# Layer 0: the q projection of the next image moved ahead of the mixing in the steps behind an image's last scores

## The chip, the cores and the metric

The kernel runs on one core of one Trainium2 chip. The metric is the device time of one execution in microseconds (us). The median of three runs is compared.

## The reference

The network has four layers, all of the form x = x + layer(group_norm(x)), on an image tensor of 4 images, 512 channels and 32x32 positions (1024 tokens), all in f32. Layer 0, in which the change lies, is an attention whose heads are mixed before the softmax:

```python
q, k, v = w_q @ xf, w_k @ xf, w_v @ xf              # 8 heads of 64 channels, 1024 tokens
attn = einsum('bhdq,bhdT->bhqT', q, k) * scale
attn = einsum('gh,bhqT->bgqT', w_head, attn)        # every head becomes a sum over all 8
attn = softmax(attn, axis=-1)
attn = (attn - mean) / sqrt(var + EPS) * in_gamma + in_beta   # one mean and var per image and head
out = einsum('bhqT,bhdT->bhqd', attn, v).reshape(b, t, c) @ w_proj.T + b_proj
```

Layer 1 is a small gate per channel, layer 2 a plain attention, and layer 3 a read of a memory of 2048 rows by the eight best matches. They are not touched.

## The kernel before

Layer 0 handles one image after the other (`for b in range(B)`). An image is cut into 32 steps of 32 queries each (`STEPS` = 32). A block of 32 queries goes through these stages, spread over several steps of the loop:

- `scores(b, s, n)` multiplies q and k for two halves of the keys (L467). ScalarE copies the result out of PSUM into the tile `ss` (L473). After the second half, eight DMAs (four issued by SyncE, four by GpSimd, L482) carry `ss` into `s2` with the heads brought next to each other on the partitions.
- Two steps later (`MIX` = 2), `mix(b, s - 2)` multiplies `s2` with the head weights (L493), `exps` takes the exponentials on ScalarE (L500), `turn_keys` transposes 32x32 blocks on VectorE (L506), and `reduce` takes sums and squares there (L521).
- Seven steps later (`LAG` = 7), `apply(b, s - 7)` multiplies a quarter of the keys of a group of four blocks with v and adds them up in the one PSUM bank `pv_bank` (L532). After the fourth quarter `take_out` copies the bank out on ScalarE (L592), and the next group may start in it. `scale` on GpSimd (L605) and a store follow.

Because of these lags seven steps, 32 to 38, have no scores any more: they only mix (steps 32 and 33, for the blocks 30 and 31) and apply. In the first four of them, 32 to 35, the kernel also makes the q projection of the next image, one of four blocks of 128 channels in each step. The function passed in as `piece` does this: `take_q(b + 1, m, s + 1)` runs 8 matmuls of 128x512 (shown as 16 records, L192, through `project`), and `put_q` copies the result with ScalarE (L292). Behind the last image the projection is that of layer 2, `take_q2`, and its result is taken by VectorE (L989). The weights come in four blocks of columns (`load_columns`, L261), asked for in steps 30 to 33 on ScalarE's DMA queue. The normalised input of the next image, `xn_all`, gets its last quarter from ScalarE at the end of step 31 (L397).

The big PSUM tiles are three, `pairs[0..2]`, used in turn: the projection of step s writes `pairs[(s + 1) % 3]`, and the mixing of step s writes `pairs[(s + 2) % 3]` and `pairs[s % 3]`.

`mid` stands between the mixing and the `piece` of a step. In the steps 32 to 38 it takes one part of the gate of layer 1 for the image before (`gating`, L145, L155, L886 and so on), so it is empty for the first image.

The order is written by hand: `pin` keeps an instruction in program order on its engine, and nearly all of layer 0 is pinned. So TensorE, ScalarE and VectorE each take the work in the order of the code below.

Of the kernel before, what the change touches and what calls it, by code (L numbers as in the profile page):

```python
# [41 lines left out]
def fast_net(ctx: ExitStack, tc: tile.TileContext, a: dict, out: bass.AP, flag: bass.AP):  # L42
# [181 lines left out]
    STEPS = T // NS  # L224
# [193 lines left out]
    def take_v(b, t):  # L418

        I = img[b]  # L420
        if t == 0:
            I["v"] = big("v", f"v0_{b}").rearrange("p k (i c) -> p (k i) c", c=C)
        ps = small_ps(f"v_{b}_{t}")
        for k in range(KC):
            pin(nc.tensor.matmul(  # L425
                ps, I["xn"][:, k, t * P:(t + 1) * P], I["w_v"][:, k, :],
                start=(k == 0), stop=(k == KC - 1),
            ))
        pin(nc.scalar.copy(I["v"][:, t, :], ps))
# [11 lines left out]
    def sum_v(b):  # L441

        I = img[b]
        vk = I.pop("vk")
        ps = small_ps(f"vt_{b}")
        for g in range(NH):
            for half in range(2):
                pin(nc.tensor.matmul(
                    ps[half * HD:(half + 1) * HD, g:g + 1],
                    vk[:, g * HD:(g + 1) * HD], ones[:, 0:1], start=True, stop=True))  # L450
        vsum = I["vsum"] = small.tile([P, NH], F32, tag="vsum", name=f"vsum{b}")
        pin(nc.vector.tensor_scalar_mul(vsum, ps[:, 0:NH], float(T)))
# [3 lines left out]
    def scores(b, s, n):  # L456


        I = img[b]
        q, k_ = I["q"], I["k"]  # L460
        if n == 0:
            I["ss", s] = eight_k([P, 2, T], f"ss_{b}_{s}", s % 2)
        ss = I["ss", s]
        sc = pairs[(s + n) % 3]
        for m in range(KC):
            for r in range(2):
                pin(nc.tensor.matmul(  # L467
                    sc[m * NS:(m + 1) * NS, r, :],
                    q[r * HD:(r + 1) * HD, m, s * NS:(s + 1) * NS],
                    k_[r * HD:(r + 1) * HD, m, n * NB:(n + 1) * NB],  # L470
                    start=True, stop=True,
                ))
        pin(nc.scalar.copy(ss[:, :, n * NB:(n + 1) * NB], sc))  # L473
        if n == 0:
            return
        s2 = I["s2", s] = apool.tile([P, 2, T], F32, tag="s2", bufs=2, name=f"s2_{b}_{s}")
        del I["ss", s]
        for r in range(2):
            for i in range(2):
                for side in range(2):  # L480
                    m = 2 * side + i
                    pin(relays[side].dma_start(  # L482
                        out=s2[2 * m + r::NH], in_=ss[m * NS:(m + 1) * NS, r, :]))
# [5 lines left out]
    def mix(b, s):  # L489
        s2 = img[b].pop(("s2", s))  # L490
        for t in range(4):
            for r in range(4):
                pin(nc.tensor.matmul(  # L493
                    mixed(s, r // 2)[t * NS:(t + 1) * NS, r % 2, :].rearrange("p (qq k) -> p qq k", qq=2),
                    wmix[r * NS:(r + 1) * NS], s2[r * NS:(r + 1) * NS, :, t * NK:(t + 1) * NK],
                    start=True, stop=True,
                ))

    def exps(s, half):
        pin(nc.scalar.activation(  # L500
            e[:, half].rearrange("p r qq k -> p (r qq k)"), flat2(mixed(s, half)), AF.Exp))

    def turn_keys(s, half):

        j, i = divmod(s, 4)
        pin(nc.vector.transpose(  # L506
            eT[:, j % 2].rearrange("p b (qq i r) x -> p i r qq b x", qq=2, i=4)[
                :, i, 2 * half:2 * half + 2],
            e[:, half].rearrange("p r qq (b x) -> p r qq b x", x=NS),
        ))  # L510

    def reduce(b, s, half):

        I = img[b]
        j, i = divmod(s, 4)
        if i == 0 and half == 0:
            I["st", j] = apool.tile([P, 4, 4, 2, 6], F32, tag="st", bufs=2, name=f"st_{b}_{j}")
        st = I["st", j]
        for r in range(2):
            for qq in range(2):  # L520
                pin(nc.vector.bn_stats(st[:, i, 2 * half + r, qq, :], e[:, half, r, qq, :]))  # L521

    def apply(b, s):

        I = img[b]
        j, part = divmod(s, 4)
        pv = pv_bank.rearrange("p (gp q) -> p gp q", q=P)
        for t in (2 * part, 2 * part + 1):
            for gp in range(KC):
                for r in range(2):  # L530
                    g = 2 * gp + r
                    pin(nc.tensor.matmul(  # L532
                        pv[r * HD:(r + 1) * HD, gp, :],
                        I["v"][:, t, g * HD:(g + 1) * HD],
                        eT[:, j % 2, t, :, 4 * g:4 * g + 4],
                        start=(t == 0 and gp == 0), stop=(t == TC - 1),
                        skip_group_check=True,
                    ))
# [51 lines left out]
    def take_out(b, j):  # L590
        pv = img[b]["pv"] = apool.tile([P, KC, P], F32, tag="o1", name=f"pv_{b}_{j}")
        pin(nc.scalar.copy(pv.rearrange("p gp q -> p (gp q)"), pv_bank))  # L592
# [94 lines left out]
    def piece_out(b, m, n):  # L687
        pin(nc.sync.dma_start(
            out=x1[b][:, m, n * NB:(n + 1) * NB], in_=img[b].pop(("xr", m, n))))
# [18 lines left out]
    def unit(i):  # L708

        return i // 2 % KC, i // (2 * KC)  # L710
# [569 lines left out]
    def step(b, s, mid, piece):  # L1280


        I = img[b]
        old = s - MIX
        mixing = 0 <= old < STEPS
        js, at = divmod(s - SUM, 4)
        if js >= TC:
            js, at = TC - 1, s - SUM - 4 * (TC - 1)
        summing = js >= 0
        j, part = divmod(s - LAG, 4)  # L1290
        tiled = 0 <= j < TC
        putting = b > 0 and OUT <= s < OUT + 16
        if b > 0 and OUT < s <= OUT + 16 and s % 2 == 0:
            piece_out(b - 1, *unit(s - 2 - OUT))
        if s == 0:
            take_v(b, 0)
        if s < STEPS:
            scores(b, s, 0)
            early(b, s)
            scores(b, s, 1)  # L1300
        else:
            early(b, s)
        if summing and at == 2:
            next(I["tail"])
        if putting:
            mid(b, s)
        if s >= MIX and "late" in I:
            turn_keys(I["late"], 1)
            reduce(b, I.pop("late"), 1)
        if summing and at == 0:  # L1310
            I["rest"] = I.pop("tail", None)
            I["tail"] = sums(b, js)
            next(I["tail"])
        if s == LAG:
            sum_v(b)
        if tiled:
            apply(b, s - LAG)
        else:
            piece(b, s)
        if mixing:  # L1320
            mix(b, old)
            exps(old, 0)
            exps(old, 1)
            turn_keys(old, 0)
        if tiled and part == 3:
            take_out(b, j)
        if b > 0 and OUT <= s + 1 < OUT + 16 and s % 2:
            image_piece(b - 1, *unit(s + 1 - OUT))
        if not putting:
            mid(b, s)  # L1330
        if s < STEPS:
            feed(b, s)
        if tiled:
            piece(b, s)
        if mixing:
            reduce(b, old, 0)
            I["late"] = old
        if summing and at >= 2:
            next(I["tail"])
        if summing and at == 0 and js > 0:  # L1340
            next(I["rest"])
        if tiled and part < 3 and j > 0:
            next(I["scale"])
        if tiled and part == 3:
            I["scale"] = scale(b, j)
# [5 lines left out]
    def early(b, s):  # L1351

        for load in state["plan"].get(s, ()):
            load()

    def mid(b, s):
        before = b - 1
        if b > 0:
            if s == 3:
                state["norm"] = instance_norm(before)  # L1360
            if 3 <= s < 7:
                next(state["norm"])
            if s in (OUT - 2, OUT - 1, OUT + 6, OUT + 7):
                norm_quarter(before, s % 2 + 2 * (s > OUT))
        if TC < s <= TC + 4 or s in (NEXT - 4, NEXT, NEXT + 2, NEXT + 3):
            next(state["ahead"])
        next(state["behind"], None)

    def piece(b, s):
        if s < TC - 1:  # L1370
            take_v(b, s + 1)
        elif b > 0 and OUT <= s < OUT + 16:
            put_quarter(b - 1, s - OUT)
# [10 lines left out]
    for b in range(B):  # L1384
# [8 lines left out]
        for s in range(STEPS):  # L1393
            step(b, s, mid, piece)
# [854 lines left out]
```

## Time and profile before

| | |
|---|---|
| median of 3 runs | 2590.84 us (2585.73 to 2593.91) |
| the profiled execution | 2590.89 us, its span 2589.2 us |
| TensorE busy | 2534.9 us, 98% of the span |
| VectorE, GpSimd, ScalarE busy | 1549.0, 1204.8, 988.4 us |
| share of TensorE in the chain that ended last | 74% |
| mixing on TensorE (L493) | 160.6 us busy, 9.3 us idle before it |

The span is the time from the first to the last instruction of the profiled execution; its own device time is 1.7 us longer. The idle time before a group is what its engine stood still just before the instructions of that group. Records of matmuls overlap, since TensorE is pipelined, so the distance from one group's start to the next group's start is a better measure of what a group costs than its length.

The steps 32 to 38 lie, on TensorE, at about 268 to 315 us for the first image, 557 to 603 us for the second, 847 to 894 us for the third and 1138 to 1185 us for the fourth.

### The profile page before, as it was taken

How to read it: one execution, taken by the hardware profiler on the slowest of the kernel's cores; microseconds unless marked ns; L12 is line 12 of the kernel's file. 1: busy time of each engine (PE TensorE's matmuls, PEld its weight loads, DVE VectorE, ACT ScalarE, POOL GpSimd, SP SyncE). 2: the span in 40 equal slices, each digit the busy share in tenths (PEclk: the TensorE clock that was granted, in tenths of full speed). 3: DMA queues.
4: the chain of work that ended last, by engine and by line, in shares of the span. 5: the costliest groups of instructions: out<-in, count | busy, mean ns of one | idle time of the engine just before them, and what ended most of it. 6: DMA issues, size and time to landing. Idle time of an engine off the chain costs nothing.

```text
span 2589.2 us, 47488 instructions
## 1 busy us (share of the span) xinstructions
PE 2534.9 (98%) x18438; PEld 1164.4 (45%) x18438; DVE 1549.0 (60%) x2668; ACT 988.4 (38%) x1165; POOL 1204.8 (47%) x1700
## 2 busy tenths in 40 slices
PE   8999999999999999999999999999999999999998
PEld 3344534544355534545533433443343344444445
DVE  4599348871788338880366147226514647787885
ACT  1467336651666236651152145025314622121211
POOL 3266315552456425543284047017404617656665
PEclk9999999999999999999999999999999999999999
DMA  2578448872698439883300120030012036767665
GB/s 82 144 208 233 119 120 233 234 205 81 179 242 235 111 95 224 234 253 122 130 17 24 68 91 21 29 134 25 13 57 82 22 113 183 224 181 222 183 189 169
DMA packets 186969, 358.22 MB, mean 138 GB/s; under 512 B 32873, under 2 KB 96361, under 8 KB 183026
## 3 DMA queue, kind: packets, MB, share of 16 engines
q1 hardware_dynamic: 105504, 175.57, 21.9%
q0 software_dynamic: 49152, 142.79, 20.3%
q10 hardware_dynamic: 32082, 36.76, 5.0%
q8 instruction: 148, 2.42, 0.4%
q14 instruction: 83, 0.68, 0.1%
HBM read 186.96 MB, written 33.82 MB: 85 GB/s over the span
## 4 chain that ended last, share of the span: by engine, by line
PE 74%; issue 10%; POOL 8%; DMA 3%; ACT 2%; DVE 2%; SPq 0%; POOLq 0%; ACTq 0%; DVEq 0%
PE pair L192 10%; PE sc_c L1027 9%; PE pv_c L1064 8%; PE pv L532 8%; POOL got L1204 7%; PE pair L467 6%; PE pair L493 5%; PE pt L425 4%; PE p L192 4%; PE pt L721 4%; PE k L192 3%; PE q L192 3%; PE v L204 3%; DMA s<-ss 2%; ACT e L500 2%
## 5 line engine op out<-in xcount | busy, mean ns | idle before, releaser
L482 POOL DMA_DIRECT2D s<-ss x512 | 259.2, 513 | 396.2 <-PE pair L493 106.4
L506 DVE STREAM_TRANSPOSE eT<-e 128x1024 f32<-128x1024 f32 x256 | 316.4, 1236 | 176.9 <-ACT e L500 176.4
L1204 POOL DMA_INDIRECT got<-in_mem,ix x256 | 279.7, 1093 | 213.3 <-DVE tmx L1210 144.3
L1021 ACT ACTIVATE eT<-sc_c 128x1024 f32<-128x1024 f32 x256 | 247.8, 1022 | 289.9 <-PE sc_c L1027 213.6
L521 DVE BATCH_NORM_STATS2 st<-e 128x6 f32<-128x256 f32 x1024 | 350.7, 404 | 0.0
L500 ACT ACTIVATE e<-pair 128x1024 f32<-128x1024 f32 x256 | 251.1, 1022 | 181.7 <-PE pair L493 145.8
L1045 POOL TENSOR_TENSOR e<-eT 128x1024 f32<-128x1024 f32 x96 | 236.2, 2464 | 158.2 <-ACT eT L1021 123.6
L467 PE MATMUL pair<-k,q 64*32 64x512 f32 x4096 | 267.4, 598 | 12.8 <-ACT e L500 12.8
L473 ACT COPY ss<-pair 128x1024 f32<-128x1024 f32 x256 | 247.2, 1019 | 74.2 <-PE pair L467 36.6
L532 PEld LDWEIGHTS pv<-eT,v 128*64 128x64 f32 x4096 | 221.1, 137 | 76.0 <-issue 59.4
L532 PE MATMUL pv<-eT,v 128*64 128x128 f32 x4096 | 250.7, 276 | 4.3 <-ACT pv L592 4.3
L1046 DVE TENSOR_TENSOR eT<-eT,e 128x1024 f32<-128x1024 f32 x96 | 138.7, 1445 | 179.8 <-POOL e L1045 179.7
L1027 PE MATMUL sc_c<-q,k 64*128 64x512 f32 x1024 | 238.7, 606 | 2.3 <-DVE xr L684 2.3
L1041 POOL TENSOR_TENSOR eT<-eT 128x1024 f32<-128x1024 f32 x32 | 80.3, 2509 | 334.8 <-ACT eT L1021 330.9
L1064 PE MATMUL pv_c<-eT,v 128*64 128x512 f32 x1024 | 233.1, 597 | 1.5 <-DVE eT L1121 1.5
L493 PE MATMUL pair<-s,wmix 32*32 32x512 f32 x4096 | 160.6, 599 | 9.3 <-DMA s<-ss 8.3
L1251 DVE SCALAR_TENSOR_TENSOR acc<-got,et,acc 128x512 f32<-128x512 f32 x210 | 157.9, 752 | 7.5
L1027 PEld LDWEIGHTS sc_c<-q,k 64*128 64x128 f32 x1024 | 94.3, 187 | 132.2 <-issue 73.3
L1184 ACT COPY att<-at 128x1024 f32<-128x1024 f32 (+1 forms) x65 | 64.9, 999 | 217.7 <-PE at L1179 216.7
L467 PEld LDWEIGHTS pair<-k,q 64*32 64x32 f32 x4096 | 57.0, 105 | 179.9 <-ACT e L500 86.6
L1064 PEld LDWEIGHTS pv_c<-eT,v 128*64 128x64 f32 x1024 | 68.0, 137 | 138.4 <-issue 136.8
L1179 PE MATMUL at<-memT,xn_d 128*128 128x512 f32 x256 | 120.7, 594 | 0.0
(295 smaller groups left out, 3306.1 us busy)
## 6 DMA issues: line engine op xcount, KB each, us to landing
s<-ss SPq DMA_DIRECT2D x512, 128.0 KB
s<-ss POOLq DMA_DIRECT2D x512, 128.0 KB
rb<-r POOLq DMA_DIRECT2D x64, 128.0 KB
o<-o SPq DMA_DIRECT2D x32, 256.0 KB
xr<-in_x ACTq DMA_DIRECT2D x32, 256.0 KB
x<-xr SPq DMA_DIRECT2D x32, 256.0 KB
xr_c<-x SPq DMA_DIRECT2D x32, 256.0 KB
rb_c<-r SPq DMA_DIRECT2D x64, 128.0 KB
```

Source lines behind the costliest of these rows:

```text
L192: pin(nc.tensor.matmul(ps[:, n, :], w[:, k, m * P:(m + 1) * P], rhs(k, n), start=(k == 0), stop=(k == KC - 1),))
L467: pin(nc.tensor.matmul(sc[m * NS:(m + 1) * NS, r, :], q[r * HD:(r + 1) * HD, m, s * NS:(s + 1) * NS], k_[r * HD:(r + 1) * HD, m, n * NB:(n ...
L482: pin(relays[side].dma_start(out=s2[2 * m + r::NH], in_=ss[m * NS:(m + 1) * NS, r, :]))
L493: pin(nc.tensor.matmul(mixed(s, r // 2)[t * NS:(t + 1) * NS, r % 2, :].rearrange("p (qq k) -> p qq k", qq=2), wmix[r * NS:(r + 1) * NS], s ...
L500: pin(nc.scalar.activation(e[:, half].rearrange("p r qq k -> p (r qq k)"), flat2(mixed(s, half)), AF.Exp))
L506: pin(nc.vector.transpose(eT[:, j % 2].rearrange("p b (qq i r) x -> p i r qq b x", qq=2, i=4)[:, i, 2 * half:2 * half + 2], e[:, half].rea ...
L521: pin(nc.vector.bn_stats(st[:, i, 2 * half + r, qq, :], e[:, half, r, qq, :]))
L532: pin(nc.tensor.matmul(pv[r * HD:(r + 1) * HD, gp, :], I["v"][:, t, g * HD:(g + 1) * HD], eT[:, j % 2, t, :, 4 * g:4 * g + 4], start=(t == ...
L1021: pin(nc.scalar.activation(e, scs[len(es)], AF.Exp))
L1027: pin(nc.tensor.matmul(sc[:, r, :], I["k"][r * HD:(r + 1) * HD, m, t * P:(t + 1) * P], I["q"][r * HD:(r + 1) * HD, m, n * NB:(n + 1) * NB] ...
L1064: pin(nc.tensor.matmul(pv[r * HD:(r + 1) * HD, :], I["v"][:, t, h * HD:(h + 1) * HD], e[:, r, :], start=(t == 0), stop=(t == TC - 1),))
L1204: pin(nc.gpsimd.indirect_dma_start(out=got[:, i, :], out_offset=None, in_=a["mem"], in_offset=bass.IndirectOffsetOnAxis(ap=ix[:, i:i + 1], ...
```

## The change

In the steps from `STEPS` on, `piece` is called right behind `apply`, ahead of `mix`, `exps`, `turn_keys`, `take_out` and `mid`. In all other steps the order stays as it is. In the steps 36 to 38 the `piece` is empty, so the steps 32 to 35 alone change.

```diff
         if tiled:
             apply(b, s - LAG)
-        else:
+        if not tiled or s >= STEPS:
             piece(b, s)
         if mixing:
             mix(b, old)
@@ -1330,7 +1330,7 @@
             mid(b, s)
         if s < STEPS:
             feed(b, s)
-        if tiled:
+        if tiled and s < STEPS:
             piece(b, s)
         if mixing:
             reduce(b, old, 0)
```

## The prediction

> **What bounds the kernel now.** I read the page first: busy times, then the chain.
>
> ```profile
> PE 2534.9 (98%) x18438; PEld 1164.4 (45%) x18438; DVE 1549.0 (60%) x2668; ACT 988.4 (38%) x1165; POOL 1204.8 (47%) x1700
> PE 74%; issue 10%; POOL 8%; DMA 3%; ACT 2%; DVE 2%; SPq 0%; POOLq 0%; ACTq 0%; DVEq 0%
> ```
>
> TensorE is busy almost throughout and holds most of the chain. A reordering can then only win where TensorE stands still, and costs wherever it makes TensorE stand still anew. So I went to the timeline of TensorE over the steps 32 to 35 of the first image. Columns: start, length, line, shapes, records, in brackets the idle time ahead and what ended it.
>
> ```profile
> 267.85 1.97 PE L532 MATMUL pv<-eT,v 128*64 128x128 f32 x32
> 271.99 1.15 PE L493 MATMUL pair<-s,wmix 32*32 32x512 f32 x32 [2.17 <-DMA s<-ss]
> 273.07 8.83 PE L192 MATMUL pair<-xn_all,w_q 128*128 128x512 f32 x16
> 281.83 1.97 PE L532 MATMUL pv<-eT,v 128*64 128x128 f32 x32
> 283.73 1.14 PE L493 MATMUL pair<-s,wmix 32*32 32x512 f32 x32
> 284.80 7.13 PE L192 MATMUL pair<-xn_all,w_q 128*128 128x512 f32 x16
> 291.86 1.97 PE L532 MATMUL pv<-eT,v 128*64 128x128 f32 x32
> 293.76 7.13 PE L192 MATMUL pair<-xn_all,w_q 128*128 128x512 f32 x16
> 300.82 1.97 PE L532 MATMUL pv<-eT,v 128*64 128x128 f32 x32
> 302.72 7.13 PE L192 MATMUL pair<-xn_all,w_q 128*128 128x512 f32 x16
> ```
>
> Apply, mixing, projection is the order of steps 32 and 33; steps 34 and 35 have apply and projection. The mixing of step 32 waits for the relayed scores of block 30; that of step 33 waits for nothing. The same place in the other three images:
>
> ```profile
> 557.35 1.97 PE L532 MATMUL pv<-eT,v 128*64 128x128 f32 x32
> 559.79 1.15 PE L493 MATMUL pair<-s,wmix 32*32 32x512 f32 x32 [0.48 <-DMA s<-ss]
> ...
> 847.41 1.97 PE L532 MATMUL pv<-eT,v 128*64 128x128 f32 x32
> 851.09 1.15 PE L493 MATMUL pair<-s,wmix 32*32 32x512 f32 x32 [1.71 <-DMA s<-ss]
> ...
> 1137.68 1.97 PE L532 MATMUL pv<-eT,v 128*64 128x128 f32 x32
> 1141.56 1.15 PE L493 MATMUL pair<-s,wmix 32*32 32x512 f32 x32 [1.91 <-DMA s<-ss]
> ```
>
> The first projection of image 0 also took 8.83 us where the others took 7.13. The table of stretches says why (its columns: stretch, length, busy time of PE, PEld, DVE, ACT, POOL, then granted clock, DMA share, GB/s):
>
> ```profile
> 269.60:273.00 3.40, 1.23 (x36) 0.27 (x32) 3.33 (x9) 1.22 (x2) 3.27 (x6) 1.00 1.05 239
> 273.00:276.40 3.40, 3.40 (x20) 1.35 (x6) 3.40 (x8) 2.05 (x2) 1.38 (x2) 0.56 1.04 295
> ```
>
> The clock fell to about half right behind the wait. The DMA share of 1.05 says why the scores are late: the DMA engines are full here. Last, ScalarE from step 33's q copy on:
>
> ```profile
> 291.97 1.01 ACT L292 COPY q<-pair 128x1024 f32<-128x1024 f32 x1 [4.96 <-PE pair L192]
> 293.93 0.59 ACT L592 COPY pv<-pv 128x512 f32<-128x512 f32 x1 [0.95 <-PE pv L532]
> 300.93 1.01 ACT L292 COPY q<-pair 128x1024 f32<-128x1024 f32 x1 [6.41 <-PE pair L192]
> ```
>
> The copy of the pv bank in step 34 (293.93) now runs under the projection of that step (293.76 to 300.82). It is off TensorE's path only because it stands ahead of the q copy.
>
> **What the Trainium skill says.** "TensorE: Matmul & The Clock Gate", Part 1: an idle window of about 3.4 us halves the clock, and windows run freely. The trace agrees in kind: 0.56 over 3.40 us. But the gap was 2.17 us, less than a full window, and gaps of 1.71 and 1.91 us in images 2 and 3 left their projections at 7.11. The same page, "Step-by-step: what each phase is for", says that TensorE can pull weight loads ahead but keeps matmuls in program order, and that it alone of the engines reorders. The timelines of TensorE and ScalarE agree: both follow the code. So a wait stops all matmuls behind it, and a ScalarE copy behind another waits for it.
>
> **What goes away (step 32).** From apply's start to the mixing's start is 1.90 us undisturbed (281.83 to 283.73). In step 32 it is 4.14, 2.44, 3.68 and 3.88 us in the four images: 2.24 + 0.54 + 1.78 + 1.98 = 6.54 us too long. With the projection ahead, the mixing starts 7.06 us after apply's end (length of a projection from start to start, 284.80 to 291.86), which covers all four. In image 1, L145 waits a further 0.2 us for VectorE; that goes too, as L145 then also comes 7 us later. The slow clock cost (281.83 - 273.07) - 7.06 = 1.70 us. Together **8.45 us**. Otherwise the same three groups run in another order, for which I take no cost; a different handover between shapes could be 0.1 us for each of 8 steps, either way.
>
> **Does the projection wait instead?** It needs three things. Weights: by the DMA semaphores' updates in the trace, the first block of columns (L261, issued at 259.58) had landed at 264.62; in the other images at 552.81, 843.96 and 1133.92; the projection would start at about 269.8, 559.3, 849.3 and 1139.6. Input: the last quarter of xn ends on ScalarE at 270.82 (L397, 269.58 plus 1.24), about 1.05 us after apply, but only the fourth of the eight matmuls (two records each, so 7.06 / 8 = 0.88 us) reads it, 2.65 us in. The margin is 1.6 us; waiting for the whole tile at the first matmul would cost 1.05 us each, 4.2 us in all. PSUM: the projection's pair was freed by exponentials of the step before. For step 33: the mixing of step 32 starts at Q, the end of the projection; the exponential starts 1.33 us later (273.32 against 271.99) and ends at Q + 2.35. TensorE is there at Q + 1.07 + 1.90 = Q + 2.97. Margin 0.6 us; I cost it at nothing. The q copy stands ahead of that exponential on ScalarE, from Q + 0.11 to Q + 1.12, and is done before the exponential may start. The mixing of block 31 needs that step's second exponential, over 6 us earlier.
>
> **What is moved past what.** A projection is 16 records of TensorE with their weight loads and one copy; it issues no DMA. On ScalarE's queue the load of the last weight block (281.94) comes forward or stays, and is needed only at 302. SyncE and GpSimd are not passed, but wait: GpSimd's L605 needs the pv copy, 8 us later in step 34, and its next work behind that starts at 310.69, so that is covered. On VectorE the transposes of block 31 ended at 289.82 (the last one starts at 288.58 and takes 1.23), 6.1 us after their mixing's start (283.73). That mixing now starts at 269.75 + 7.06 + 1.07 + 1.90 + 7.06 = 286.84, so they end near 292.9; the apply that reads all of them starts at 296.9 at the earliest: margin 4 us. In the last image VectorE takes q (1.28 us) ahead of transposes whose exponentials come later still: nothing.
>
> **What is added (step 34).** Now `take_out` stands behind the q copy on ScalarE. The next apply (step 35) is the first of a new group and needs the bank. With TensorE's next start at 300.82: q copy at 300.93, second copy 0.92 us behind it (two ScalarE instructions of 1.02 take 1.94 together), 0.59 long, TensorE 0.05 later: 302.49. So **1.67 us** of new idle time in image 0. In images 1 and 2 the small L155 (0.25 us) falls into it: 1.42 each. In the last image q is copied by VectorE (L989), ScalarE is free, and the cost is 0. Sum: 1.67 + 2 x 1.42 = **4.5 us**. Bounds: 0 if the copy goes ahead after all, 4.5 + 3 x 1.70 = 9.6 if the clock falls behind each.
>
> **Sum.** -8.45 + 4.5 = -3.95 us. Against the profiled 2590.89 this is 2586.9; the median, 2590.84, stands at the same place.
>
> **Rivals.**
> *Only the gain:* the pv copy does not bind, 2590.84 - 8.45 = 2582.4. For it: TensorE waited for L592 only 4.3 us in all. Against it: the order of the code.
> *Slower, by the clock:* in step 34 each of three new gaps lets the clock fall for one window at 1.70 us. -8.45 + 4.5 + 5.1 = +1.1, so 2592.0; if it lasts two windows each, 2597. It decides between a gap that did no harm (1.91) and one that did (2.17), and on how it lies in the window; 1.67 speaks against it.
> *The wait changes its name:* the projection waits for all of xn, +4.2: 2591.1. Against it: the input is written and read by quarters.
> *It does nothing measurable,* because the relays' lateness reappears at a later mixing. Against it: the relays of block 31 had landed at 276.53, and its mixing would come at 287: it stays at 2586.9 then.
>
> **Numbers.** The forecast gets 0.62, only the gain 0.14, the clock 0.13, the renamed wait 0.11. 0.3% (7.8 us) is about what a measurement of this kernel can tell from no change. Most of "only the gain" and the low edge of the forecast lie below 2583.1: 0.20. Above 2598.6 lie the worst of the clock case and what I don't see, unpinned work of later layers among it: 0.09. The rest, 0.71, is within. Range 2581.5 to 2594.0: from a little below the full gain to the clock case with the spread of the runs.
>
> **What would show it.** Right: no `DMA s<-ss` wait at the mixing of steps 32, projections at 7.1, and `ACT pv L592` ahead of step 35's apply at 1.4 to 1.7 us in three images, none in the fourth. Wrong: a wait at L192 for `ACT xn_all L397` or a DMA, a granted clock of 0.5 behind step 34, or no wait at L532.

## The result, and the profile after

| | before | after |
|---|---|---|
| median of 11 runs | 2590.49 us | 2585.75 us |
| ratio to before, 95% interval | | 0.9976 (0.9966 to 0.9987) |
| the profiled execution, and its span | 2590.89, 2589.2 us | 2587.30, 2585.5 us |
| mean granted TensorE clock of the profiled execution | 0.998 | 0.999 |

The ratio of 0.9976 is 6.2 us of 2590 (3.4 to 8.8 us); the medians lie 4.7 us apart, the means 4.3 us and the two profiled executions 3.6 us. The forecast was 2586.9 us, 3.95 us under the kernel before, which lies within that interval. A second set of 9 runs, made beside the first experiments, gave 0.9968 (0.9955 to 0.9982), 8.3 us (4.7 to 11.7 us), which is more than the forecast.

The page of the kernel after, busy times and chain by engine:

```profile
PE 2533.4 (98%) x18438; PEld 1162.9 (45%) x18438; DVE 1548.0 (60%) x2668; ACT 986.9 (38%) x1165; POOL 1199.9 (46%) x1700
PE 74%; issue 8%; POOL 7%; DMA 7%; ACT 2%; DVE 1%; SPq 0%; POOLq 0%; ACTq 0%; DVEq 0%
```

TensorE still does the same 18438 matmul records in nearly the same busy time (2533.4 against 2534.9 us), and still carries the chain. Totals can't show a change of this size; the stage does. The timeline of TensorE over steps 32 to 35 of the first image, kernel after:

```profile
268.30 1.97 PE L532 MATMUL pv<-eT,v 128*64 128x128 f32 x32
270.20 7.13 PE L192 MATMUL pair<-xn_all,w_q 128*128 128x512 f32 x16
277.26 1.14 PE L493 MATMUL pair<-s,wmix 32*32 32x512 f32 x32
278.34 1.97 PE L532 MATMUL pv<-eT,v 128*64 128x128 f32 x32
280.23 7.13 PE L192 MATMUL pair<-xn_all,w_q 128*128 128x512 f32 x16
287.30 1.14 PE L493 MATMUL pair<-s,wmix 32*32 32x512 f32 x32
288.37 1.97 PE L532 MATMUL pv<-eT,v 128*64 128x128 f32 x32
290.27 7.13 PE L192 MATMUL pair<-xn_all,w_q 128*128 128x512 f32 x16
298.99 1.97 PE L532 MATMUL pv<-eT,v 128*64 128x128 f32 x32 [1.59 <-ACT pv L592]
300.89 7.13 PE L192 MATMUL pair<-xn_all,w_q 128*128 128x512 f32 x16
```

Three things are to be seen. First, the mixing of step 32 (277.26) has no wait ahead of it, and neither has the projection (270.20). Second, all four projections take 7.13 us: none runs at the slow clock. Third, the apply of step 35 (298.99) has a wait that was not there. ScalarE shows why, in the same kernel:

```profile
297.44 1.01 ACT L292 COPY q<-pair 128x1024 f32<-128x1024 f32 x1 [6.86 <-PE pair L192]
298.35 0.59 ACT L592 COPY pv<-pv 128x512 f32<-128x512 f32 x1
```

The pv copy waits its turn behind the q copy, and the apply follows it by 0.05 us (298.35 + 0.59 = 298.94). The apply of step 35 in images 1 and 2, and in the last image, from the timelines of TensorE after:

```profile
586.61 1.97 PE L532 MATMUL pv<-eT,v 128*64 128x128 f32 x32 [1.47 <-ACT pv L592]
...
877.53 1.97 PE L532 MATMUL pv<-eT,v 128*64 128x128 f32 x32 [1.47 <-ACT pv L592]
...
1166.54 1.97 PE L532 MATMUL pv<-eT,v 128*64 128x128 f32 x32
```

Two more waits, and none in the last image, where VectorE takes q.

The stage can be summed from start to start, from the apply of step 32 to the first k projection behind step 38 (times in us):

| image | before | after | difference | the prediction's terms |
|---|---|---|---|---|
| 0 | 267.85 to 315.32 | 268.30 to 313.48 | -2.29 | -2.24 - 1.70 + 1.67 = -2.27 |
| 1 | 557.35 to 603.09 | 555.61 to 602.04 | +0.69 | -0.54 - 0.2 + 1.42 = +0.68 |
| 2 | 847.41 to 894.11 | 846.53 to 892.96 | -0.27 | -1.78 + 1.42 = -0.36 |
| 3 | 1137.68 to 1185.29 | 1137.08 to 1182.63 | -2.06 | -1.98 |

The four sum to -3.93 us, against -3.95 in the prediction. For these stages of these two executions the account closes. That the whole spans differ by nearly the same amount (3.7 us) is in part luck: by the starts and ends in the table, the time outside the stages grew by 1.27 us up to the end of the last stage and shrank by 1.04 us behind it. In that last part, which the change does not touch, the two executions differ in the clock. The first matmuls of layer 2's attention wait 2.3 us in both:

```profile
1273.44 8.83 PE L1027 MATMUL sc_c<-q,k 64*128 64x512 f32 x32 [2.32 <-DVE xr L684]
...
1270.78 7.14 PE L1027 MATMUL sc_c<-q,k 64*128 64x512 f32 x32 [2.31 <-DVE xr L684]
```

The first line is of the kernel before, the second of the kernel after. In the 3.40 us from these starts the granted clock was 0.51 before and 1.00 after. So one pair of executions can't settle the size of the change, and the question stays why the second set shows more than the forecast.

### The profile page after: what moved, and what is told of

Same layout as the page of the kernel before. It is cut to its first block, busy times and chain, and to the rows that moved or that the text cites. A ratio compares the mean times of both kernels' runs of the same rounds, so it can differ in the third digit from the quotient of the medians.

```text
span 2585.5 us, 47491 instructions
## 1 busy us (share of the span) xinstructions
PE 2533.4 (98%) x18438; PEld 1162.9 (45%) x18438; DVE 1548.0 (60%) x2668; ACT 986.9 (38%) x1165; POOL 1199.9 (46%) x1700
## 4 chain that ended last, share of the span: by engine, by line
PE 74%; issue 8%; POOL 7%; DMA 7%; ACT 2%; DVE 1%; SPq 0%; POOLq 0%; ACTq 0%; DVEq 0%
PE pair L192 10%; PE sc_c L1027 9%; PE pv_c L1064 9%; PE pv L532 8%; POOL got L1204 7%; PE pair L467 6%; PE pair L493 5%; PE pt L425 4%; PE pt L721 4%; PE p L192 3%; PE k L192 3%; PE q L192 3%; PE v L204 3%; DMA got<-in_mem,ix 3%; DMA s<-ss 3%
## 5 line engine op out<-in xcount | busy, mean ns | idle before, releaser
L473 ACT COPY ss<-pair 128x1024 f32<-128x1024 f32 x256 | 247.2, 1020 | 78.6 <-PE pair L467 37.5
L1027 PE MATMUL sc_c<-q,k 64*128 64x512 f32 x1024 | 237.2, 602 | 2.4 <-DVE xr L684 2.3
L1027 PEld LDWEIGHTS sc_c<-q,k 64*128 64x128 f32 x1024 | 93.5, 186 | 131.7 <-issue 72.0
```

The costliest lines, as they stand in the source:

```text
L1027: pin(nc.tensor.matmul(sc[:, r, :], I["k"][r * HD:(r + 1) * HD, m, t * P:(t + 1) * P], I["q"][r * HD:(r + 1) * HD, m, n * NB:(n + 1) * NB] ...
```

## The experiments

Each is compared with the kernel before on the same chip. Where means are given, they are means over all its runs, and "clock" is the mean granted TensorE clock of these runs. By my estimate from these figures, a clock of 0.999 over 2590 us stands for 2.6 us lost by a TensorE that is always busy.

**The changed kernel again, and its parts.** The yardstick of the first group:

> The changed kernel once more, as the yardstick of this group. My account (a saving of 8.45 us at the mixing of step 32, a cost of 4.5 us at the apply behind step 34): 3.9 us under the kernel before. If the change gains elsewhere too, as the 4.7 us between the medians and the ratio of 0.9976 leave open: 6 us or more under it.

Measured: 0.9968 (0.9955 to 0.9982), median 2583.35 us, 8.3 us: more than my account gives. Where the rest comes from is taken up below, with step 32 alone.

The projection ahead only where there is a mixing (this edit and those below are against the kernel before unless said otherwise; `...` stands for lines left out):

```diff
-        else:
+        if not tiled or STEPS <= s < STEPS + MIX:
             piece(b, s)
...
-        if tiled:
+        if tiled and not (STEPS <= s < STEPS + MIX):
             piece(b, s)
```

> The projection stands ahead only in steps 32 and 33, where there is a mixing; steps 34 and 35 keep the old order. My account: the whole saving and none of the cost, 8.45 us under the kernel before and 4.5 us under the changed one; no wait of the apply for ACT pv L592 over 1 us. Rival (the pv copy's place costs nothing in the end, since the saved time is waited for later): the same as the changed kernel.

Measured: 0.9959 (0.9944 to 0.9974), median 2578.57 us, 4.8 us under the changed kernel's median. The waits of TensorE for the pv copy are 4.3 us in 12 places with a longest of 1.0, as in the kernel before; in the kernel after they are 8.9 us in 15 places. So the cost is close to the forecast 4.5 us, and the saving, 12.4 us by the means, is more than forecast.

The complement, with the condition `s >= STEPS + MIX` in both places:

> The projection stands ahead only in steps 34 and 35; steps 32 and 33 keep the old order. My account: only the cost, 4.5 us over the kernel before, in three waits of 1.4 to 1.7 us for ACT pv L592, none behind the last image; the mixing of step 32 waits as before. Rival: no difference from the kernel before.

Measured: 1.0021 (1.0010 to 1.0032), mean 2596.97 against 2591.76 us: 5.2 us slower (2.6 to 8.3 by the interval). The rival, no difference, falls. Its timeline of TensorE in the first image has both waits at once:

```profile
267.01 1.97 PE L532 MATMUL pv<-eT,v 128*64 128x128 f32 x32
272.06 2.02 PE L493 MATMUL pair<-s,wmix 32*32 32x512 f32 x32 [3.08 <-DMA s<-ss]
274.01 7.71 PE L192 MATMUL pair<-xn_all,w_q 128*128 128x512 f32 x16
...
302.31 1.97 PE L532 MATMUL pv<-eT,v 128*64 128x128 f32 x32 [1.59 <-ACT pv L592]
```

The apply's wait is the same 1.59 us as in the kernel after. The mixing's wait, in the old order of step 32, is 3.08 us here and was 2.17 in the profile before.

**Whose place costs.** The changed order in all four steps, with the q copy of step 34 (`m == 2`) on another engine; this edit is against the changed kernel:

```diff
-    def put_q(q, m):
+    def put_q(q, m, ahead=False):
+        if ahead:
+            return lambda ps: pin(nc.vector.tensor_copy(q[:, m, :], ps))
         return lambda ps: pin(nc.scalar.copy(q[:, m, :], ps))
...
-        project(I["w_q"], tokens(I["xn"]), m, at, put_q(I["q"], m))
+        project(I["w_q"], tokens(I["xn"]), m, at, put_q(I["q"], m, m == 2))
```

> The changed order in all four steps, but the q copy of step 34 is made by VectorE and not by ScalarE. My account (the cost is the pv copy queued behind the q copy on ScalarE): the cost is gone, 8.45 us under the kernel before, and the pv copy follows the apply of step 34 within 1 us. Rival (the cost comes from the projection's place on TensorE, whichever engine copies): as the changed kernel, 3.9 us under.

Measured: 0.9958 (0.9945 to 0.9971), median 2578.93 us, the same as without the move in step 34. ScalarE of this kernel (its lines are two further down in the file, so L594 is the pv copy):

```profile
286.30 1.94 ACT L502 ACTIVATE e<-pair 128x1024 f32<-128x1024 f32 x2 [0.23 <-PE pair L495]
288.12 0.59 ACT L594 COPY pv<-pv 128x512 f32<-128x512 f32 x1
304.06 1.01 ACT L294 COPY q<-pair 128x1024 f32<-128x1024 f32 x1 [15.34 <-PE pair L192]
```

The pv copy now comes right behind the apply of step 34 (286.03 on TensorE), under the projection, and the apply of step 35 has no wait:

```profile
294.99 1.97 PE L534 MATMUL pv<-eT,v 128*64 128x128 f32 x32
```

So the cost is not the projection's place on TensorE but the q copy's place on ScalarE: shown.

**Which step saves.** The condition `s == STEPS`, and in another kernel `s == STEPS + 1`:

> Only in step 32 does the projection stand ahead of the mixing. My account: the whole saving comes from this step, since only its mixing waits for the relayed scores: 8.45 us under the kernel before. Rival (both steps with a mixing take part): half of that or less.

Measured: 0.9953 (0.9940 to 0.9966), median 2578.84 us, mean 2578.54 against 2590.66: 12.1 us under the kernel before.

> Only in step 33 does the projection stand ahead of the mixing. My account: nothing, within 1 us of the kernel before, and the mixing of step 32 waits as before. Rival (the order in step 33 saves or costs by itself, by the handover between shapes or by exponentials that come later): 2 us or more either way.

Measured: 0.9999 (0.9987 to 1.0010). So step 32 makes the whole saving, and step 33 nothing that can be told (3 us either way). Its size is 12 us (8.8 to 15.5) and not 8.45. Two things can make up the difference.

First, the wait varies from execution to execution. Three profiled kernels have the old order in step 32. What lies between the starts of apply and mixing beyond the undisturbed 1.90 us, summed over the four images: 6.54 us before, 7.42 in the kernel that moves step 33 only (2.29, 1.80, 2.24, 1.09), 11.80 in the one that moves steps 34 and 35 only (3.15, 4.14, 1.81, 2.70). The mean is 8.6. It may be high, since the last two executions took 4.3 and 7.3 us more than the means of their kernels. The profile names other releasers than the relays for three of these twelve waits (`ACT xn_all L397`, or "issue"); by the semaphores' updates in the traces the last relay had landed 0.4 to 0.7 us before the mixing there too, as it had where the relays are named.

Second, the clock. In these three profiles it falls in or behind one, two and three of the four waits. Averaged over runs, the granted clock is 0.9977 in the kernel before (40 runs) and 0.9992 with step 32 moved (5 runs): 0.0015 of 2590 us, 3.9 us. Together 8.6 + 3.9 = 12.5 us, against 12.1 measured. The same sum for the change as it was made: 8.6 less the 4.5 of step 34 is 4.1; its clock is 0.9986 in the first set of runs and 0.9989 in the second, so 2.4 to 3.1 us; 6.5 to 7.2 us, between the two measured figures of 6.2 and 8.3. The sums agree better than a mean of three profiles and the clock of five runs can promise. That all of the 3.9 us lies at step 32 is not shown: these three profiles hold two or three slow stretches elsewhere in the kernel too (in the kernel before at about 1273 and 2577 us), and the profile with step 32 moved holds none but at its very end.

**Why the relays are late.** The kernel before, with less in the DMA engines ahead of them:

```diff
-        plan |= {NEXT + 2 + m: [load_columns(b, key, a[key], m)] for m in range(KC)}
+        plan |= {NEXT + 3 + m: [load_columns(b, key, a[key], m)] for m in range(KC)}
```

> The kernel before, with the four weight columns of the next projection asked for one step later each (steps 31 to 34). My account of why the relayed scores of block 30 are late (the DMA engines are full, share 1.05): 256 KB less stand ahead of them, about 1 us at the 239 GB/s of that stretch, so the waits at the mixing of step 32 fall by about 1 us each where they were 1.7 to 2.2, and the kernel is 2 to 4 us faster. Rival (a fixed latency of the relays from the last scores on): the waits stay as they are.

Measured: 0.9976 (0.9968 to 0.9984), 6.2 us, more than the 2 to 4 expected and as much as the change itself. Step 32 loses 1.37, 2.10, 0.86 and 1.33 us in its profile, 5.66 in all, 2.9 under the mean of the three above; the clock of its runs is 0.9987, 2.5 us better than before. A latency that is fixed from the last scores on would not shorten when a load of weights is put off. From the end of the copy of block 30's last scores (L473) to its mixing it was 10.50, 11.33, 11.18 and 11.26 us in the four images of the profile before, and is 9.64, 11.49, 10.26 and 10.73 us here. It is not fixed, and three of the four are shorter, so that rival falls; the forecast fall of about 1 us for each wait is not seen in every image. How much of the wait is the bytes ahead in the engines and how much the rate they share is not told apart.

Both remedies at once:

> The projection ahead of the mixing in step 32 only, and the weight columns asked for one step later each: both remedies for the late relays at once. My account: they cure the same wait, so the second adds nothing, 12 us under the kernel before as with the first alone; and the projection, which now starts at about 268 us in the first image, comes close to the landing of its first weights (268.7 for a load asked for in step 31 in the profile before), so a wait of up to 1 us at L192 in each image can appear, for a result up to 4 us worse than the first alone. Rival (the two gains add up): 18 us under the kernel before.

Measured: 0.9966 (0.9957 to 0.9975), 8.8 us under the kernel before: the gains do not add up to the 18 us of the rival, and the result is no better than with step 32 alone. TensorE at the projection of step 32, first and last image:

```profile
268.31 7.10 PE L192 MATMUL pair<-xn_all,w_q 128*128 128x512 f32 x16 [0.91 <-DMA w_q<-in_w_q]
...
1132.77 7.10 PE L192 MATMUL pair<-xn_all,Wq 128*128 128x512 f32 x16 [1.26 <-DMA Wq<-in_Wq]
```

With its weights a step later the projection itself has to wait. This is the wait that the prediction ruled out by the landing times; it comes when the weights are asked for one step later.

**How long a gap lowers the clock.** The changed kernel, with the q copy of step 34 made twice by ScalarE, the second time over the first:

> The changed kernel, with the q copy of step 34 made twice in a row by ScalarE behind the first three images. My account: the wait for the pv copy grows by 0.92 us in each of three images, to about 2.6, 2.4 and 2.4 us; 2.8 us over the changed kernel by the waits alone. If gaps of 2 us and more bring the clock down as in the profile before: up to 1.7 us more for each that lies in one window of the clock, and the granted clock shows 0.5 behind it. Rival (such gaps never lower the clock, the slow stretch before had another cause): 2.8 us and no more.

Measured: 0.9995 (0.9985 to 1.0006), mean 2589.95 us. The two sets of the changed kernel have a mean of 2584.74, so the doubling costs about 5.2 us; these sets stood in other groups of runs, where the kernel before had means of 2590.1 and 2591.8 against 2590.7 here. From start to start the gaps grow by 1.05 us each (the start of the projection to the start of the next apply is 9.77 us, against 8.72 after), 3.15 in all; the clock is 0.9977 against 0.9988, a further 2.7 us. The table of stretches around the gap of image 2 (columns as in the prediction):

```profile
870.60:874.00 3.40, 3.40 (x9) 1.49 (x9) 1.13 (x4) 0.00 (x0) 1.01 (x4) 1.00 0.00 0
874.00:877.40 3.40, 0.88 (x10) 0.56 (x10) 0.16 (x1) 2.51 (x3) 1.52 (x3) 1.00 0.00 0
877.40:880.80 3.40, 3.40 (x33) 3.07 (x29) 0.00 (x0) 0.00 (x0) 1.44 (x2) 0.52 0.00 0
```

A stretch with TensorE busy for 0.88 of 3.40 us is followed by one at 0.52, in which the apply took 3.33 us where it takes 1.97. The DMA share is 0.00 here, so full DMA engines are not needed for a slow clock. In this profile only one of the three gaps (2.63, 2.52 and 2.52 us) lowered the clock. So the rival, that such gaps never do it, falls; and the price is a chance for each gap, not a fixed sum.

## Why the prediction was right, and where it was short

- **The bound.** TensorE carried the time, and only its gaps moved. Held.
- **What goes away in step 32.** The mechanism held in each of the four images to 0.1 us between the two profiled executions, and step 32 alone makes the saving. But the term was mis-sized: 6.54 us came from one execution, where three profiles give 6.5 to 11.8 us.
- **The slow clock, 1.70 us.** This was the step that failed in size. I counted the one slow stretch that the profile before happened to hold in these stages. Over the runs the clock of the kernel before stands for 2590 x 0.0023 = 6.0 us lost in the whole kernel, and with step 32 moved 3.9 of them are won back, in the stages or elsewhere. The page's row of granted clock, in tenths, shows none of this.
- **Does the projection wait instead?** It did not, by any of the three needs. The weights' lead was needed: with the weights a step later a wait of 0.9 to 1.3 us appeared in two images of that profile.
- **What is added in step 34.** 1.67 and twice 1.42 us forecast; from start to start it is 8.72 - 7.06 = 1.66 us in image 0, and 1.42 in images 1 and 2 with L155's 0.24 taken off; none in the last. Its cause was shown twice, by leaving the step alone and by copying q on VectorE.
- **Rivals.** "Only the gain" was wrong for this change: the new waits are there. The clock case did not come about (no slow stretch behind step 34 in either of its two profiles), though with the doubled copy one of three gaps brought it. The argument against it, that 1.67 us is shorter than a gap that did no harm (1.91), does not hold as a rule, since a wait of 1.53 us brought a slow stretch in another profile (shown in the last section). That none came in six gaps may be luck in part. The renamed wait and "nothing measurable" are excluded by the timeline after.
- **The range.** Both medians of the changed kernel lie within 2581.5 to 2594.0, below its middle, which fits the terms that were sized too small. That the first lies only 1.2 us from the forecast 2586.9 is partly luck: by the means against the kernel before of the same set, the change won 4.3 us in the first set and 8.4 us in the second.

The versions that leave step 34 in the old order, or copy its q on VectorE, beat both kernels, with medians of 2578.6 to 2578.9 us.

## What to carry to other kernels

A block of independent work put in front of a matmul that waits for a transfer hides the wait; but the block's copy out of PSUM goes into a queue too, and what stands behind it there (here a copy that frees a bank) is the price. Look up the queue of every engine that the moved block uses, not only the one where the wait was. And size a wait that ends with a DMA from several executions: the same four waits gave 6.5 us in one profile and 11.8 in another, with a slow clock behind one of them and behind three.

## What the runs showed of the hardware that was not expected

- A gap on TensorE that is well under 3.4 us was enough for a stretch of about 3.4 us at half clock, if not each time, and the length of the gap alone does not decide. Such stretches stand behind waits of 2.17 us (kernel before) and 2.52 us (doubled copy), while waits of 1.71 and 1.91 us left the next projection at 7.11 us, and waits of 2.52 and 2.63 us in the profile with the doubled copy did no harm either. In the kernel that moves step 33 only, a wait of 1.53 us ahead of an earlier mixing was followed by one:

```profile
1010.21 3.04 PE L493 MATMUL pair<-s,wmix 32*32 32x512 f32 x32 [1.53 <-DMA s<-ss]
...
1007.80:1011.20 3.40, 1.87 (x22) 0.81 (x16) 2.99 (x8) 1.02 (x2) 3.07 (x7) 1.00 0.96 189
1011.20:1014.60 3.40, 3.40 (x33) 1.45 (x32) 0.14 (x1) 2.10 (x3) 1.72 (x4) 0.51 0.81 192
```

- One and the same gap is hit or missed. The 2.3 us wait ahead of layer 2's attention (L1027, lower in the versions with added lines), which no version touches, stands in all eleven profiles. Behind it the granted clock was 0.50 to 0.54 in four of them, and the matmuls took 8.69 to 8.83 us; it was 1.00 in seven, and they took 7.14 us.
- The granted clock of the kernel before differs between executions, from 0.995 to 0.999 over 40 runs, with a mean of 0.9977. Over these runs a clock lower by 0.001 goes with about 2.7 us more (correlation -0.78), so a good part of the scatter between runs goes with the clock. That gaps of this kind make that part is likely from the profiles, but not shown for the runs that were not profiled.
